# Four graph layers on one core: W a on TensorE, another beginning, and layer 2 projecting before it aggregates

## The chip, the cores and the metric

The kernel runs on one core of one Trainium2 chip. The metric is the device time of one execution in microseconds; the median of three runs is given. One execution was also recorded by the hardware profiler, and all views of the profile are of that one.

## The reference

There are 64 graphs of 256 nodes with 512 features. Each has an adjacency matrix `adj` (256 x 256) with positive weights and ones of its own on the diagonal. Four layers follow each other, each of the form `x = x + L(relu(layernorm(x)), adj)`. All is f32.

```
L0: Wh = h W0;  e[i,j] = leaky_relu((Wh a1)[i] + (Wh a2)[j]);  masked where adj <= 0.5
    att = softmax(e over i);   elu(att Wh)
L1: A = adj + I;  d = rsqrt(rowsum A);   relu((d A d) h W1 + b1)
L2: relu(adj h W2) * (row of h's input is not all zero)
L3: agg = (adj h) / max(rowsum adj, eps);   relu([h, agg] W3^T)
```

## The kernel before, in words

**One product.** A 256 x 256 result over 256 inner rows is formed by seven products of halves instead of eight, after Winograd. The seven left blocks are named A11, A12, S1, A22, S2, S4, S3, the seven right ones B11, B21, B22, T1, T2, T3, T4N. S and T are sums and differences of the other blocks. The weights' blocks (`wb[0]` to `wb[4]`, four layers and the two halves of W3) are made once at the beginning: `weight()` loads four blocks of 256 KB, `weight_sums()` makes T1 to T4N on GpSimd; `last_weight()` turns W3 by TensorE transposes.

**One graph.** `graph(b)` records the operations of a graph. `x` stays in the tile `xs`, the adjacency comes twice: `a_nat` as it is, for row sums, and by eight DMAs in blocks of 32 (`ab`) that VectorE turns into `aT`. A layer is: `norm(l)` (sums on GpSimd and ScalarE, then `h` on ScalarE); `aggregate(h, moving, l)`, which forms (A h)^T in two PSUM banks by 8 matmuls of 256 columns; `left_sums()`, which copies the four blocks into the tile `xw` (ScalarE, VectorE) and calls `more_sums()` for S2, S3 and S4 (VectorE, GpSimd); and `project()`, seven products with the layer's weights, each of two 128-row chunks, in three PSUM banks `pz`, `pv`, `py`. After a product, ScalarE copies a bank to a kept tile (`plain_keep`) or VectorE adds it to one (`plain_total`). Then comes the layer's nonlinearity and the addition to `xs` (`elu0`, `relu_add`, `masked`).

**Layer 0** makes the two logit vectors on VectorE as sums of `h0 * wa`, where `wa` holds W0 a. The first vector is needed along the free axis; `along()` brings it there: a small VectorE transpose, a DMA to DRAM (`dpl`) and a DMA back to all partitions (`pl`). `wa` itself is made at the beginning by `logit_weights()`: W0 is loaded once more, `a` is loaded in 128 copies, VectorE makes eight products with sums, and TensorE spreads the columns.

**Layer 3** projects before it aggregates. h^T is needed as left operand: VectorE transposes `h3` within blocks of 32 into `hb`, and 16 DMAs of 32 KB put the blocks in place in `hw`, in runs of 128 bytes. Then `hw` is multiplied by the neighbours' half of W3 (`wb[4]`, seven products) into the tile `y`, VectorE and GpSimd form y's T blocks, and seven products with 128-row blocks of `aT` and their sums `aw` (class `Gathered`) are accumulated into the same banks as the seven with `wb[3]`.

**Order.** Each operation is recorded with an engine, a declared time, and keys that it reads and writes. `Plan.place()` then walks through all operations of all graphs, with a list of buffers by tag, and fixes one static order per engine: the operation that can start first by the declared times (multiplied by `STRETCH`), then the urgent one, then the one with the earliest due time. Graph b's due time is `APART * b`, with an advance for the last `LAST` graphs. `SPARE` is added to a TensorE operation's ready time. All DMAs are issued by SyncE, in that order. So several graphs are under way at once, and TensorE's stream mixes their products.

Of the kernel before, what the change touches and what calls it, by code (L numbers as in the profile page):

```python
# [14 lines left out]
P = 128  # L15
Q = 32
# [6 lines left out]
APART = 12.0  # L23
LAST, LATE = 2, 0.3

STRETCH = {"DVE": 1.25, "ACT": 1.15, "POOL": 1.2, "PE": 1.0, "DMA": 1.0}
SPARE = 0.15
# [122 lines left out]
def kernel(  # L150
# [39 lines left out]
    class Tiles:  # L190
# [5 lines left out]
        def declare(self, name, shape, pool=None, tag=None):  # L196
            tag = pool or tag or name
            self.tiles[name] = Buffered(shape, tag, f"{name}_{self.name}")
# [43 lines left out]
    def spread(to, col):  # L242

        nc.tensor.transpose(to, col.to_broadcast([P, P]), ident)
# [8 lines left out]
    def logit_weights():  # L253
        me = Tiles("l", 0.0)
        op, declare = me.op, me.declare
        declare("wa_col", [P, 2, FC])
        for k in range(FC):
            declare(f"w0{k}", [P, O], tag="xw")
            op("DMA", 256, lambda g, k=k: nc.sync.dma_start(  # L259
                g[f"w0{k}"], w0[k * P : (k + 1) * P, :]), (), [f"w0{k}"])  # L260
        for j in range(2):
            declare(f"a{j}", [P, O], tag="ex512")
            op("DMA", 256, lambda g, j=j: nc.sync.dma_start(
                g[f"a{j}"],
                a0[j * O : (j + 1) * O, :].rearrange("o u -> u o").to_broadcast([P, O])),
               (), [f"a{j}"])
        for k in range(FC):
            for j in range(2):
                declare(f"junk{j}{k}", [P, O], tag="mva")
                op("DVE", 0.77, lambda g, j=j, k=k: nc.vector.scalar_tensor_tensor(  # L270
                    g[f"junk{j}{k}"], g[f"w0{k}"], 1.0, g[f"a{j}"], ALU.mult, ALU.mult,
                    accum_out=g["wa_col"][:, j, k : k + 1]),
                   [f"w0{k}", f"a{j}"], [f"junk{j}{k}", f"wa_col.{j}"])
        for j in range(2):
            declare(f"pw{j}", [P, F], "ps")

            def go(g, j=j):
                for k in range(FC):
                    spread(g[f"pw{j}"][:, k * P : (k + 1) * P], g["wa_col"][:, j, k : k + 1])

            op("PE", 0.6, go, [f"wa_col.{j}", "=ident"], [f"pw{j}"])
            op("ACT", 0.59, lambda g, j=j: nc.scalar.copy(wa[:, j, :], g[f"pw{j}"]),
               [f"pw{j}"], [f"=wa{j}"])

    def weight_sums(op, n, b12):
        w = wb[n]
        key = lambda i: b12 if i is None else f"=wb{n}.{i}"
        part = lambda g, i: g[b12] if i is None else w[:, i]
        for to, i, j in ((T1, None, B11), (T2, B22, T1), (T3, B22, None), (T4N, B21, T2)):
            op("POOL", 1.28, lambda g, to=to, i=i, j=j: nc.gpsimd.tensor_tensor(  # L290
                w[:, to], part(g, i), part(g, j), ALU.subtract),
               [key(i), key(j)], [key(to)])

    def weight(n, w):

        me = Tiles(f"w{n}", 0.0)
        me.declare("b12", [P, FH, OH], tag="hb")
        for at, i, j in ((B11, 0, 0), (None, 0, 1), (B22, 1, 1), (B21, 1, 0)):
            block = w[i * FH * P : (i + 1) * FH * P, j * OH : (j + 1) * OH].rearrange(
                "(k p) o -> p k o", p=P  # L300
            )
            me.op("DMA", 256, lambda g, at=at, block=block: nc.sync.dma_start(
                g["b12"] if at is None else wb[n][:, at], block),
                  (), ["b12" if at is None else f"=wb{n}.{at}"])
        weight_sums(me.op, n, "b12")

# [32 lines left out]
    def quarter(t, i, j):  # L339
        return t[:, i, j * OH : (j + 1) * OH]  # L340

    def graph(b):
# [82 lines left out]

        def more_sums(xw):
            put = lambda *n: [f"{xw}.{i}" for i in n]
            op("DVE", 0.43, lambda g: nc.vector.tensor_tensor(  # L428
                g[xw][:, S2], g[xw][:, S1], g[xw][:, A11], ALU.subtract),
               put(S1, A11), put(S2), urgent=True)  # L430
            for i, o in ((A22, S3), (A12, S4)):
                op("POOL", 0.85, lambda g, i=i, o=o: nc.gpsimd.tensor_tensor(  # L432
                    g[xw][:, o], g[xw][:, i], g[xw][:, S2], ALU.subtract),
                   put(i, S2), put(o), urgent=True)
# [39 lines left out]
        class Weighted:  # L474
# [5 lines left out]
            def left(self, g, at, k):  # L480
                return g[self.x][:, at, k]
# [114 lines left out]


# [34 lines left out]
        along("pl", lambda g: g["lg"][:, 0, :], ["lg.00", "lg.01"])  # L632
# [25 lines left out]
        aggregate("h0", "e", 0)  # L658
# [17 lines left out]
        project([Weighted("xw0", 0)], 0, plain_keep, 0.38, plain_total, lambda _: elu0(*first, "a"))  # L676
        elu0(*second, "b")
        elu0(*third, "c")
# [54 lines left out]
        aggregate("h2", "aT", 2)  # L733
# [12 lines left out]
        project([Weighted("xw2", 2)], 2, plain_keep, 0.38, plain_total, lambda _: masked(*first, "a"))  # L746
# [9 lines left out]

        declare("hb", [P, NC, F])
        for c in range(NC):
            op("DVE", 0.71, lambda g, c=c: nc.vector.transpose(g["hb"][:, c, :], g["h3"][:, c, :]),
               [f"h3.{c}"], [f"hb.{c}"])  # L760
        declare("hw", [P, 7, FH, P], tag="xw")
        parts = [(a, q) for a in range(P // Q) for q in range(P // Q)]
        for a, q in parts:
            op("DMA", 32, lambda g, a=a, q=q: nc.sync.dma_start(
                g["hw"][q * Q : (q + 1) * Q, : 2 * NC].rearrange("j s k n -> j (s k) n")[
                    :, :, a * Q : (a + 1) * Q],
                g["hb"][a * Q : (a + 1) * Q].rearrange("j c (k q r) -> q j (c k) r", q=P // Q, r=Q)[q]),
               ["hb.0", "hb.1"], [f"hw.{a}{q}"], holds=0.7)
        op("DVE", 0.43, lambda g: nc.vector.tensor_tensor(
            g["hw"][:, S1], g["hw"][:, S1], g["hw"][:, A22], ALU.add),  # L770
           [f"hw.{a}{q}" for a, q in parts], [f"hw.{i}" for i in (A11, A12, A22, S1)], urgent=True)
        more_sums("hw")

        declare("y", [P, 7, OH], tag="xw")
        declare("y12", [P, OH], tag="ex256")
        places = {(0, 0): (lambda g: g["y"][:, B11], f"y.{B11}"),
                  (0, 1): (lambda g: g["y12"], "y12"),
                  (1, 1): (lambda g: g["y"][:, B22], f"y.{B22}")}
        project([Weighted("hw", 4)], 4, plain_keep, 0.38, plain_total,
                lambda pz: op("ACT", 0.38, lambda g: nc.scalar.copy(g["y"][:, B21], g[pz]),  # L780
                              [pz], [f"y.{B21}"], urgent=True), places=places)
        for eng, us, to, i, j in (("DVE", 0.43, T1, None, B11), ("POOL", 0.85, T3, B22, None),
                                  ("DVE", 0.43, T2, B22, T1), ("DVE", 0.43, T4N, B21, T2)):
            name = lambda n: "y12" if n is None else f"y.{n}"
            of = lambda g, n: g["y12"] if n is None else g["y"][:, n]
            on = nc.vector if eng == "DVE" else nc.gpsimd
            op(eng, us, lambda g, on=on, to=to, i=i, j=j: on.tensor_tensor(
                g["y"][:, to], of(g, i), of(g, j), ALU.subtract), [name(i), name(j)],
               [f"y.{to}"], urgent=True)

        declare("aw", [P, 4, P], tag="mva")
        block = lambda g, c, i: g["aT"][:, c, i * P : (i + 1) * P]
        op("POOL", 0.5, lambda g: nc.gpsimd.tensor_tensor(
            g["aw"][:, 0], block(g, 0, 1), block(g, 1, 1), ALU.add), ["aT"], [f"aw.{S1}"])
        op("POOL", 0.5, lambda g: nc.gpsimd.tensor_tensor(
            g["aw"][:, 1], g["aw"][:, 0], block(g, 0, 0), ALU.subtract),
           ["aT", f"aw.{S1}"], [f"aw.{S2}"])
        for at, to, i in ((2, S3, 1), (3, S4, 0)):
            op("POOL", 0.5, lambda g, at=at, i=i: nc.gpsimd.tensor_tensor(
                g["aw"][:, at], block(g, 1, i), g["aw"][:, 1], ALU.subtract),  # L800
               ["aT", f"aw.{S2}"], [f"aw.{to}"])
        project([Weighted("hw", 3), Gathered("aT", "aw", "y")], 3, plain_keep, 0.38, plain_total,
# [9 lines left out]
    logit_weights()  # L812
# [4 lines left out]
    for b in range(B):  # L817
        graph(b)
    buffers = dict(
        xs=7, a_nat=1, ab=1, aT=6, h=3, mva=6, xw=5, c=3, off=1, junk=1, ex256=3, ex512=2,  # L820
        wa_col=1, turned=1, row=4, pl=1, pr=1, hb=1, ps=8,
# [37 lines left out]
```

## Time and profile before

| | |
|---|---|
| median of three runs | 2843.36 us (2842.63 to 2843.51) |
| profiled execution | 2844.11 us, its span 2842.3 us |
| granted TensorE clock, mean | 0.999 |
| PE / DVE / ACT / POOL busy | 2802.9 / 1963.5 / 1691.1 / 1246.4 us |
| matmul instructions | 12968 |
| mean busy share of the 16 DMA engines, queue q1 | 24.0% |
| moved | 161.07 MB in 495062 packets, 424816 of them under 512 B |
| SyncE: time of one h^T transfer's issue (`hw<-hb`, x1024) | 609 ns median |

PE is TensorE's matmul stream and PEld its weight loads, which overlap it; DVE is VectorE, ACT ScalarE, POOL GpSimd, SP SyncE. An f32 product is two matmul instructions, so instruction counts are twice the products of the code, but for the transposes. L529 is the line of the product matmuls in `project`, L460 that of `aggregate`. A tile's name in a row has its numbers left out: `hw` is h^T of layer 3, `xw` the aggregated and summed blocks of layers 0 to 2, `wa_col_l` and `junk_l` belong to `logit_weights`.

### The profile page before, as it was taken

How to read it: one execution, taken by the hardware profiler on the slowest of the kernel's cores; microseconds unless marked ns; L12 is line 12 of the kernel's file. 1: busy time of each engine (PE TensorE's matmuls, PEld its weight loads, DVE VectorE, ACT ScalarE, POOL GpSimd, SP SyncE). 2: the span in 40 equal slices, each digit the busy share in tenths (PEclk: the TensorE clock that was granted, in tenths of full speed). 3: DMA queues.
4: the chain of work that ended last, by engine and by line, in shares of the span. 5: the costliest groups of instructions: out<-in, count | busy, mean ns of one | idle time of the engine just before them, and what ended most of it. 6: DMA issues, size and time to landing. Idle time of an engine off the chain costs nothing.

```text
span 2842.3 us, 43136 instructions
## 1 busy us (share of the span) xinstructions
PE 2802.9 (99%) x12968; PEld 2461.2 (87%) x12968; DVE 1963.5 (69%) x5136; ACT 1691.1 (59%) x4115; POOL 1246.4 (44%) x2331
## 2 busy tenths in 40 slices
PE   5999999999999999999999999999999999999999
PEld 4888888888888888888888888888888888888887
DVE  7767676676766767667676667676776766667654
ACT  5766566556666566566565665665665656556552
POOL 6554344444444444444444444444444444443432
PEclk9999999999999999999999999999999999999999
DMA  7122331222222222222222222222222222222112
GB/s 199 20 51 61 72 70 40 62 53 53 58 53 58 56 49 59 61 45 61 46 62 56 47 66 55 48 59 56 53 59 47 60 53 40 58 49 44 39 34 52
DMA packets 495062, 161.07 MB, mean 57 GB/s; under 512 B 424816, under 2 KB 460656, under 8 KB 494832
## 3 DMA queue, kind: packets, MB, share of 16 engines
q1 hardware_dynamic: 494832, 158.33, 24.0%
q8 instruction: 105, 1.72, 0.3%
q14 instruction: 125, 1.02, 0.1%
HBM read 90.96 MB, written 33.69 MB: 44 GB/s over the span
## 4 chain that ended last, share of the span: by engine, by line
PE 97%; DMA 1%; DVE 1%; POOL 0%; SPq 0%; issue 0%; ACT 0%; DVEq 0%; POOLq 0%
PE pz L529 43%; PE pt L460 23%; PE pv L529 21%; PE py L529 11%; POOL wb L290 0%; DMA xs<-in_x_dram 0%; DMA ab<-in_adj_dram 0%; DVE e L628 0%; SPq L603 0%; DMA wb<-in_L_gnn_W_dram 0%; DVE e L642 0%; DMA pr<-dpr 0%; DVE xw L445 0%; SPq L259 0%; DVE stats L385 0%
## 5 line engine op out<-in xcount | busy, mean ns | idle before, releaser
L529 PE MATMUL pz<-wb,xw 128*128 128x256 f32 x3072 | 767.9, 379 | 2.5 <-DVE c L694 0.6
L529 PEld LDWEIGHTS pz<-wb,xw 128*128 128x128 f32 x3072 | 582.9, 190 | 83.9 <-ACT c L568 1.1
L568 ACT COPY c<-pz 128x256 f32<-128x256 f32 x576 | 213.6, 371 | 550.9 <-PE pz L529 550.3
L529 PE MATMUL pz<-wb,hw 128*128 128x256 f32 x2048 | 524.8, 379 | 0.9 <-ACT c L568 0.9
L432 POOL TENSOR_TENSOR xw<-xw 128x256 f32<-128x256 f32 x384 | 296.1, 791 | 482.1 <-DVE xw L428 326.5
L529 PEld LDWEIGHTS pz<-wb,hw 128*128 128x128 f32 x2048 | 389.0, 190 | 54.5 <-ACT c L568 1.7
L422 ACT ACTIVATE h<-xs,nb,rstd 128x512 f32<-128x512 f32 x512 | 402.1, 809 | 45.5 <-POOL nb L419 39.7
L529 PE MATMUL pv<-wb,xw 128*128 128x256 f32 x1536 | 393.7, 379 | 1.7 <-DVE xw L445 1.1
L529 PEld LDWEIGHTS pv<-wb,xw 128*128 128x128 f32 x1536 | 291.5, 190 | 41.9 <-POOL wb L290 1.5
L570 DVE TENSOR_TENSOR c<-pv,c 128x256 f32<-128x256 f32 x384 | 161.7, 421 | 222.3 <-PE pv L529 150.4
L401 ACT ACTIVATE h<-xs,mv 128x512 f32<-128x512 f32 x384 | 275.4, 718 | 56.1 <-POOL mv L395 36.3
L529 PE MATMUL pv<-wb,hw 128*128 128x256 f32 x1024 | 262.8, 379 | 0.0
L460 PE MATMUL pt<-e,h 128*128 128x256 f32 x1024 | 233.8, 381 | 15.8 <-ACT e L655 15.8
L460 PE MATMUL pt<-aT,h 128*128 128x256 f32 x1024 | 236.9, 379 | 0.0
L460 PE MATMUL pt<-ahT,h 128*128 128x256 f32 x1024 | 233.1, 379 | 0.0
L460 PEld LDWEIGHTS pt<-e,h 128*128 128x128 f32 x1024 | 195.8, 191 | 43.0 <-ACT e L655 16.1
L409 POOL TENSOR_TENSOR rstd<-rstd,minus_half 128x2 f32<-128x2 f32 x256 | 215.9, 843 | 17.3
L460 PEld LDWEIGHTS pt<-aT,h 128*128 128x128 f32 x1024 | 194.5, 190 | 26.7 <-ACT h L422 0.3
L460 PEld LDWEIGHTS pt<-ahT,h 128*128 128x128 f32 x1024 | 194.6, 190 | 26.5
L529 PEld LDWEIGHTS pv<-wb,hw 128*128 128x128 f32 x1024 | 194.5, 190 | 26.5
L628 DVE SCALAR_TENSOR_TENSOR e<-h,wa 128x512 f32<-128x512 f32 x256 | 196.7, 768 | 16.5 <-ACT h L422 5.8
L529 PE MATMUL py<-wb,xw 128*128 128x256 f32 x768 | 197.1, 379 | 0.0
(116 smaller groups left out, 4460.8 us busy)
## 6 DMA issues: line engine op xcount, KB each, us to landing
xs<-in_x_dram SPq DMA_DIRECT2D x64, 512.0 KB
hw<-hb SPq DMA_DIRECT2D x1024, 32.0 KB
out_dram<-xs SPq DMA_DIRECT2D x64, 512.0 KB
ab<-in_adj_dram SPq DMA_DIRECT2D x512, 32.0 KB
a_nat<-in_adj_dram SPq DMA_DIRECT2D x64, 256.0 KB
pl<-dpl SPq DMA_DIRECT2D x64, 128.0 KB
pr<-dpr SPq DMA_DIRECT2D x64, 128.0 KB
w3n_w<-in_L_gnn_W_dram SPq DMA_DIRECT2D x4, 512.0 KB
```

Of the source, the lines that this page charges most:

```text
L401: op("ACT", 1.0, lambda g, c=c: nc.scalar.activation(g[h][:, c, :], g["xs"][:, c, :], AF.Square, bias=g[mv][:, 0, c : c + 1], accum_out=g[ ...
L409: op("POOL", 0.72, lambda g: nc.gpsimd.tensor_tensor(g[rs], g[rs], minus_half, ALU.pow), [rs, "=half"], [rs])
L422: op("ACT", 0.81, lambda g, c=c: nc.scalar.activation(g[h][:, c, :], g["xs"][:, c, :], AF.Relu, bias=g[nb][:, c : c + 1], scale=g[rs][:, c ...
L432: op("POOL", 0.85, lambda g, i=i, o=o: nc.gpsimd.tensor_tensor(g[xw][:, o], g[xw][:, i], g[xw][:, S2], ALU.subtract), put(i, S2), put(o), ...
L460: nc.tensor.matmul(g[pt][:, kk, :], lhsT=g[h][:, c, k * P : (k + 1) * P], rhs=g[moving][:, c, :], start=(c == 0), stop=(c == NC - 1),)
L529: nc.tensor.matmul(g[t], lhsT=o.left(g, left, k), rhs=o.right(g, right, k), start=start and n == 0, stop=n == len(parts) - 1, skip_group_c ...
L568: return "ACT", lambda g, to, block: nc.scalar.copy(to, block)
L570: plain_total = (0.43, lambda g, i, to, block: nc.vector.tensor_tensor(to, block, to, ALU.add))
L628: op("DVE", 0.77, lambda g, j=j, c=c: nc.vector.scalar_tensor_tensor(g["e"].rearrange("p c n -> p (c n)"), g["h0"][:, c, :], 1.0, wa[:, j, ...
```

## The change

Five things change.

- W a: `logit_weights()` takes the blocks of W0 that are loaded anyway, transposes them on TensorE (16 transposes), loads `a` as eight rows of 128 (4 KB), transposes these, and forms W a by eight matmuls of 512 columns with a broadcast column as weights. The second load of W0, the 128 copies of `a` and VectorE's eight products go.
- The beginning: graphs 0 and 1 (`FIRST = 2`) do layer 0 in the other order: TensorE transposes h, the projection makes `wh`, and then two products of 512 columns for each half of the nodes aggregate it. Graphs 0 to 2 (`ON_PE = 3`) spread the logit row by two TensorE transposes in place of `along()`.
- Layer 2 does as layer 3's neighbours: `turn(2)` makes h^T by the DMAs, `neighbours(2, 2)` projects it with `wb[2]`, `block_sums` makes the sums of `aT`, and seven products `Gathered` aggregate. `aggregate` and `left_sums` of layer 2 go.
- `turn()`, for layers 2 and 3: VectorE's transposes write the two node halves woven (node 0 of half 0, node 0 of half 1, and so on), so that the 16 DMAs move runs of 256 bytes. The blocks A11, A12, S1 and A22 of `hw` therefore have a step of two words; S2, S3 and S4 are packed.
- The planner's constants and buffers: APART 12 to 16, LAST 2 to 4, LATE 0.3 to 0.5, STRETCH of DVE 1.25 to 1.15, of ACT 1.15 to 1.0, of POOL 1.2 to 1.25, SPARE 0.15 to 0.3; aT 6 to 7 buffers, mva 6 to 5, ex256 3 to 4, ex512 2 to 1.

```diff
+    def logit_weights(me):
+        OC = O // P
+        op("DMA", 4, lambda g: nc.sync.dma_start(
+            g["a_rows"], a0.rearrange("(r p) u -> r (p u)", p=P)), (), ["a_rows"])
+        op("PE", 0.15, lambda g: nc.tensor.transpose(
+            g["pa"], g["a_rows"], ident[: 2 * OC, : 2 * OC]), ["a_rows", "=ident"], ["pa"])
...
+                    nc.tensor.transpose(
+                        g[f"pw{i}"][:, k * P : (k + 1) * P], block[:, k % FH, o : o + P], ident)
...
+                op("PE", 0.9, lambda g, i=i, j=j: nc.tensor.matmul(
+                    g[f"pwa{j}"],
+                    lhsT=g["a_cols"][:, j * OC + i : j * OC + i + 1].to_broadcast([P, P]),
+                    rhs=g[f"wt{i}"], start=i == 0, stop=i == OC - 1,
...
+        def woven(t):
+            return t[:, : 4 * FH].rearrange("p b n -> p (b n)").rearrange(
+                "p (s k n i) -> p s k n i", s=2, k=FH, i=NC)
+        def left(t, at, k):
+            if len(t.shape) == 4:
+                return t[:, at, k]
+            if at < 4:
+                return woven(t)[:, at % 2, k, :, at // 2]
+            return t[:, at * FH + k]
...
+        def turn(l):
+            declare(hb, [P, F // Q, Q, NC], tag="hb")
+            for c in range(NC):
+                op("DVE", 0.71, lambda g, c=c: nc.vector.transpose(
+                    g[hb][:, :, :, c], g[h][:, c, :].rearrange("p (k r) -> p k r", r=Q)),
+                   [f"{h}.{c}"], [f"{hb}.{c}"])
+            declare(hw, [P, 7 * FH, P], tag="xw")
+            for a, q in parts:
+                op("DMA", 32, lambda g, a=a, q=q: nc.sync.dma_start(
+                    woven(g[hw])[q * Q : (q + 1) * Q, :, :, a * Q : (a + 1) * Q].rearrange(
+                        "j s k n i -> j (s k) (n i)"),
+                    g[hb][a * Q : (a + 1) * Q].rearrange("j (k q) r c -> q j k (r c)", q=P // Q)[q]),
+                   [f"{hb}.0", f"{hb}.1"], [f"{hw}.{a}{q}"], holds=0.42)
...
-        along("pl", lambda g: g["lg"][:, 0, :], ["lg.00", "lg.01"])
+        if b < ON_PE:
+            declare("pl", [P, N], "ps")
+            op("PE", 0.23, lambda g: [
+                spread(g["pl"][:, c * P : (c + 1) * P], g["lg"][:, 0, c : c + 1]) for c in range(NC)
+            ], ["lg.00", "lg.01", "=ident"], ["pl"])
+        else:
+            along("pl", lambda g: g["lg"][:, 0, :], ["lg.00", "lg.01"])
...
-        aggregate("h0", "e", 0)
+        if b < FIRST:
+                        nc.tensor.transpose(
+                            g[pt][:, k, c * P : (c + 1) * P], g["h0"][:, c, f0 : f0 + P], ident)
+            left_sums("pt0_0", "pt0_1", "xw0")
+            project([Weighted("xw0", 0)], 0, plain_keep, 0.38, plain_total, ..., places=places)
+            for i, piece in ((1, second), (0, third)):
+                        nc.tensor.matmul(g[po], lhsT=g["e"][:, c, i * P : (i + 1) * P],
+                            rhs=g["wh"][:, c, :], start=c == 0, stop=c == NC - 1)
...
-        aggregate("h2", "aT", 2)
+        turn(2)
+        neighbours(2, 2)
+        block_sums(2, "aT")
-        project([Weighted("xw2", 2)], 2, plain_keep, ...)
+        project([Gathered("aT", "aw2", "y2")], 2, plain_keep, ...)
...
+        turn(3)
+        neighbours(3, 4)
+        block_sums(3, "aT")
+        project([Weighted("hw3", 3), Gathered("aT", "aw3", "y3")], 3, plain_keep, ...)
```

## The prediction

> **What bounds the kernel now.** I read the busy row and the slices of the page first, then a table of stretches, then the waits of PE, then groups by shape, and last the start as a timeline.
>
> ```profile
> PE 2802.9 (99%) x12968; PEld 2461.2 (87%) x12968; DVE 1963.5 (69%) x5136; ACT 1691.1 (59%) x4115; POOL 1246.4 (44%) x2331
> PE   5999999999999999999999999999999999999999
> PEclk9999999999999999999999999999999999999999
> ```
>
> TensorE is full at full clock in 39 of 40 slices. No other engine is above 69%.
>
> ```profile
> 0.00:34.00 34.00, 4.56 (x10) 2.16 (x11) 21.27 (x55) 10.11 (x23) 17.23 (x25) 1.00 0.82 241
> 34.00:60.00 26.00, 23.18 (x104) 18.43 (x104) 24.14 (x52) 17.27 (x50) 21.59 (x31) 1.00 0.71 191
> 500.00:2500.00 2000.00, 2000.00 (x9268) 1760.61 (x9268) 1399.20 (x3663) 1201.76 (x2915) 867.39 (x1642) 1.00 0.24 54
> 2790.00:2843.00 53.00, 46.48 (x213) 39.93 (x212) 22.23 (x49) 11.38 (x28) 7.88 (x12) 0.97 0.23 60
> ```
>
> The columns after the length are PE, PEld, DVE, ACT, POOL (busy, instructions), then clock, DMA share and GB/s. Between 500 and 2500 us PE has no idle time: 2000 / 9268 = 0.2158 us for one 256-column matmul instruction. Each 256-column f32 product is two of them (x1024 in 64 graphs for the 8 products of an aggregation), so one product costs 0.4316 us. All 12928 layer instructions take 12928 x 0.2158 = 2789.9 us, the 32 transposes of W3 about 3.5 (eight took 0.87). The span of 2842.3 therefore holds 48.9 us that are not layer work, nearly all at its two ends.
>
> ```profile
> PE pt L460 <- ACT e L655: 15.8, 1, 15.8
> PE pw_l L244 <- DVE junk_l L270: 13.2, 5, 9.5
> ```
>
> These are PE's only long waits: for W a, and for the first attention matrix.
>
> **Steady state, the saving.** Layer 2 now aggregates (8 products of 256 columns) and then projects (7 x 2 = 14): 22. Changed, it projects (14) and gathers in seven products: 21. A graph goes from 101 to 100. In graphs 0 and 1 the aggregation of layer 0 becomes four products of 512 columns, equal to eight. So 64 x 0.4316 = 27.6 us leave the engine that has no gap.
>
> **What it adds, and what hides it.** All rows are per instruction of the same work in layer 3.
>
> ```profile
> L759 DVE STREAM_TRANSPOSE hb<-h 128x512 f32<-128x512 f32 x128 | 86.6, 693 | 0.3 <-ACT h L422 0.2
> L787 DVE TENSOR_TENSOR y<-y 128x256 f32<-128x256 f32 x128 | 80.0, 625 | 19.0 <-ACT y L780 16.2
> L787 POOL TENSOR_TENSOR y<-y,y 128x256 f32<-128x256 f32 x64 | 61.1, 955 | 55.8 <-DVE y L570 52.5
> L529 PEld LDWEIGHTS pz<-wb,hw 128*128 128x128 f32 x2048 | 389.0, 190 | 54.5 <-ACT c L568 1.7
> L244 PEld LDWEIGHTS pw_l<-ident,wa_col_l 128*128 128x128 f32 x8 | 1.4, 181 | 15.6 <-issue 9.5 <-DVE junk_l L270 6.1
> ```
>
> DVE gains per graph two transposes (1.4), three additions into y (3 x 0.42), three differences (2 x 0.625 + 0.43) and slower block sums (0.596 + 0.567 for 0.414 + 0.455, +0.3): 4.6 us. It had 1963.5 / 64 = 30.7 of 44.4 us and gets 35.3 of about 43.2, 82%. ACT gains four copies of 0.371 and loses 0.589 + 0.372: +0.5, to 62%. POOL gains T3 (0.955) and the four sums of a^T (0.507 + 0.473 + 2 x 0.55): +3.0, to 52%. None reaches PE, so I price them at 0. If the cover fails, each 0.1 us of PE waiting per graph costs 6.4 us.
>
> The transposes write, and the block sums and weight loads read, every second word now. No row of before has such an access. For DVE and POOL the ends are the same time and double: the transposes of layers 2 and 3 would add 2.8 us, DVE would be at 88%, still below PE.
>
> SP issues 32 transfers of h^T per graph in place of 16. One holds it for a median of 609 ns now, at 256 runs of 128 bytes; the row vector pl, 128 runs, holds it 368. With 128 runs of 256 bytes I take 0.37 to 0.61: 11.8 to 19.5 us in place of 9.7. The rest of SP's issues is about 7 us (ab 3.8 in the timeline, seven others at 0.35 to 0.57), so at most 26.5 of 43.2. What stands behind them on SP is x, ab and a_nat of later graphs, with about a graph's time of lead. The DMA engines are at 24%; the number of packets of h^T stays, their size doubles. Even at double time per packet they would not pass 40%.
>
> The Trainium skill, "DMA: Bandwidth & Descriptors" (Specifications), speaks against runs this short: line rate needs 512 bytes or more. By it both 128 and 256 are poor. No row here separates the two, and at this share it would change no term.
>
> Does the new latency of layer 2 fit? From layer 1's last sum: relu 0.73, POOL mean 0.38, two squares 1.8, POOL 0.24 + 0.84 + 0.22, two h 1.6, two transposes 1.4, 16 issues 5.9 to 9.7, landing 3.5 (last issue over at 1004.25, first sum on hw at 1007.70), sum 0.6: 17 to 21 us, some 3 more for hand-overs. In the changed order at least 34 us of other graphs' PE instructions stand there for graphs 6 to 57 (count x 0.2158), and 30 ahead of layer 3. From the neighbours' last v product to T2's use lie at least 3.0 us; the need is 0.42 + 0.43 + 0.62 and hand-overs, about 2. It fits, but with far less room than at the turn.
>
> **The start.**
>
> ```profile
> 16.01 0.25 DVE L355 STREAM_TRANSPOSE tpl<-lg 128x64 f32<-128x64 f32 x1
> 21.88 0.34 SPq L361 DMA_DIRECT2D pl<-dpl  x1
> 26.22 0.91 ACT L634 ACTIVATE e<-pl,lg 128x256 f32<-128x256 f32 x2 [0.34 <-DMA pl<-dpl]
> 33.20 5.62 PE L460 MATMUL pt<-e,h 128*128 128x256 f32 x16 [15.84 <-ACT e L655]
> ```
>
> Now the first layer work begins at 33.2; the row of logits alone travels 10 us through DRAM. Changed, W0 is loaded once and not twice, a as 4 KB and not 512 KB: 1.8 MB stand up to graph 0's ab, at 241 GB/s about 8 us plus issue, and I put ab at 12 and h at 14.6 (now 14.9). PE's W a costs 17 transposes at 0.11 and eight 512-column products of 0.863, 8.8 us, all in idle time; it ends near 17, no earlier than now (18.0). DVE loses eight products of 0.68, 5.4 us. The gain is elsewhere: eight transposes of h (0.9) and the projection can run from 18 to 25 while the softmax is made, and the logits take two spreads (0.47 each in the row of the eight for W a) in place of the 10 us. In the changed order e waits behind aT of graph 1 on DVE (its ab cannot be issued before graph 0's aT is read, so near 21), then min, top, exp, division, with two h of graph 1 between: ready near 28.5. The two 1.7 us aggregations follow.
>
> By 60 us PE now has done about 87 layer instructions and 20 transposes, 21 us of work. Changed, I count by then two projections of layer 0 (12), their aggregations (6.9), the next layer 0 and two layer 1 aggregations (10.4), one projection of layer 1 (6) and the W3 transposes (3.5): 38.8. That is 17.8 us ahead. DVE was 24.14 of 26 busy from 34 to 60 and has more to do per graph now, so part is given back before steady state. Ends: 0 and 18. I take 11.
>
> **The end.** The last PE product now feeds an addition (0.42) and a 512-wide relu (0.69) before the store; changed, its last feeds one relu of 0.42: -0.7. The last four graphs are packed otherwise, and layer 2 has a longer chain there: +0 to +6, with new short gaps elsewhere; I take +2.
>
> **Sum.** 2844.1 (profiled execution; its span is 2842.3, 1.8 around it) - 27.6 - 11 - 0.7 + 2 = 2806.8. The median of the runs lies 0.75 lower: 2806.
>
> **Rivals.** *Strided weights, slower than before.* Left blocks A11, A12, S1 and A22 are loaded with every second word: 4 of 7 products, two chunks, two instructions, three projections, 48 instructions per graph, 3072 in all. A load takes 190 ns under a matmul step of 215.8. It is free up to there; beyond, each pays the excess. It eats the whole gain at 215.8 + 39.3 / 3.072 = 229 ns, a load 20% longer; at double, 380, it costs 504 us: 3310. Against it: the load of a broadcast column, step 0, took 181, not more than a packed one. I take 0, the row nearest to it being any load there is. Chance 0.08.
> The Trainium skill, "SBUF — State Buffer" (the note on 16-byte cachelines), says that reads keep full speed while two fall in one line, for f32 up to a step of 8 bytes or so; by it this price is 0. No run here shows it yet.
>
> *DVE's queue.* At 82% and in order, an addition that PE's next product needs may come late in every graph. For: the ends above. Against: apart from W a, PE waited for DVE 2.4 us in all of before. With 0.2 to 0.4 us per graph the time is 2819 to 2832 (0.08); over 0.6 it is no gain or worse (0.07, of which 0.02 stay within the bound).
>
> *The new beginning brings nothing*, since DVE is the bound until 100 us: 2806 + 11 = 2817. Chance 0.15.
>
> **Numbers.** The forecast itself 0.62. What a measurement can tell from no change is about 0.2%, 5.7 us. Faster 0.62 + 0.15 + 0.08 = 0.85; same 0.02; slower 0.05 + 0.08 = 0.13. The range goes from 18 us at the start and no cost at the end (2806 - 7 - 2 = 2797, three less for that sum's errors) to near the end of the late-DVE case: 2794 to 2830.
>
> **What would show it.** 100 products per graph and a step of 215.8 ns with no idle PE between 500 and 2500; loads on hw of 190 ns; layer work of graph 0 before 20 us and the first aggregation near 28; DVE near 82%. It is wrong if loads on hw pass 216 ns, if PE's waits name DVE y or DMA hw by the hundred, or if PE shows gaps after 100 us.

## The result and the profile after: 7% slower, with gaps in front of layers 2 and 3

The changed kernel takes 3043.43 us (median of 4 runs, 3042.51 to 3047.97) against 2843.2: a ratio of 1.0707, interval 1.0691 to 1.0722. The forecast was 2806. The profiled execution took 3043.74 us, its span is 3041.9, the mean granted clock 0.991.

The busy row, TensorE's slices and the shares of the chain that ended last, from the page of the changed kernel:

```profile
PE 2857.0 (94%) x12871; PEld 2456.7 (81%) x12871; DVE 2157.4 (71%) x5623; ACT 1718.8 (57%) x4246; POOL 1450.0 (48%) x2653
PE   8899899999999999999999999999999999999998
...
SPq 36%; PE 33%; DVE 10%; DMA 8%; issue 6%; POOL 4%; ACT 3%; DVEq 0%; ACTq 0%; POOLq 0%
```

The slices hide it: a nine stands for 90% and up. The busy row shows it: TensorE has 3041.9 - 2857.0 = 184.9 us of idle time where before had 39.4. That is +145.5; the other 54.1 of the 199.6 us by which the span grew are busy time, although there are fewer instructions. Part of that goes with the clock (0.991 where before had 0.999; 0.8% of 2857 is 23 us, an estimate). The rest is longer instructions, the products on h^T among them (389 ns in the mean, 379 in the run with four transfers below); how it divides is not shown. The chain says more: SyncE's issues hold 36% of it. In before TensorE held 97%.

The stretch of 2000 us that had no gap before:

```profile
500.00:2500.00 2000.00, 1900.40 (x8629) 1643.26 (x8628) 1447.33 (x3797) 1151.10 (x2850) 954.57 (x1770) 1.00 0.29 63
```

With 200 instructions to a graph, a graph takes 2000 / 8629 x 200 = 46.4 us. Without gaps it would take 200 x 0.2158 = 43.2; before it took 43.6. So the saving per graph is there and 3.2 us lie on top, 2.3 of gaps and 0.9 of longer instructions, 64 times over: 205 us.

What TensorE, SyncE's queue and VectorE wait for (total us, times, longest):

```profile
PE pzy L565 <- DMA hw<-hb: 116.4, 87, 3.1
PE pzy L565 <- ACT y L604: 15.1, 14, 1.4
PE pzy L565 <- issue: 9.8, 17, 1.4
```

```profile
SPq L645 <- PE pz L565: 358.6, 67, 11.5
SPq L907 <- DVE xs L847: 219.9, 41, 13.5
SPq L645 <- DVE hb L639: 206.6, 47, 12.5
```

```profile
DVE hw L650 <- DMA hw<-hb: 470.4, 127, 5.7
```

`pzy` are the first products on h^T, and they wait 87 times for its transfers. That comes near the "by the hundred" that the prediction named as a sign against it, and the gaps after 100 us, another of its signs, are there. The second table tells what SyncE's queue waits for. 47 times a turn waits for VectorE's transposes of h, which the prediction had counted. 67 times it waits for a TensorE product: `hw` shares its five buffers (`xw`) with the aggregated blocks and with `y`, and SyncE can't write into one before the last product has read its former contents. The row of L907 is the wait for a finished graph before it is stored. The last row is the largest wait for the transfers: in 127 of 128 turns VectorE comes to the first sum on `hw` before the data and stands there, 3.7 us in the mean. Its work for the other graphs, and the next transposes of h with it, stands behind that sum. In before the same wait was 4.3 us in all.

One turn in the order of time (start, length, engine, line):

```profile
1035.01 1.31 DVE L639 STREAM_TRANSPOSE hb<-h 128x512 f32<-128x512 f32 x2
...
1038.04 10.26 SPq L645 DMA_DIRECT2D hw<-hb  x16
...
1049.93 0.43 DVE L650 TENSOR_TENSOR hw<-hw 128x256 f32<-128x256 f32 x1 [4.43 <-DMA hw<-hb]
1049.96 1.11 PE L565 MATMUL pzy<-wb,hw 128*128 128x256 f32 x4 [0.83 <-DMA hw<-hb]
```

h^T is transposed in its blocks at 1036.3; SyncE then waits 1.6 us for a `pz` product, the issue begins at 1038.0 and lasts 10.3 us, and the last piece lands 1.6 us after it. VectorE has stood for 4.4 us and TensorE for 0.8, and both start at once. The order was built for 16 x 0.42 = 6.7 us of issue. One transfer takes:

```profile
L645 SPq DMA_DIRECT2D hw<-hb x2048: 585/599/1861, 87.8 to 3011.4; - x187
```

599 ns median (between minimum and maximum), where the 256 runs of 128 bytes of before took 609. Half the number of runs made it 2% shorter. The `holds=0.42` of the diff is what the planner was told; before told it 0.7 for 0.609.

### The profile page after: what moved, and what is told of

It reads as the page before. It is cut to its first block, busy times and chain, and to the rows that moved or that the text cites. A ratio compares the mean times of both kernels' runs of the same rounds, so it can differ in the third digit from the quotient of the medians.

```text
span 3041.9 us, 45682 instructions
## 1 busy us (share of the span) xinstructions
PE 2857.0 (94%) x12871; PEld 2456.7 (81%) x12871; DVE 2157.4 (71%) x5623; ACT 1718.8 (57%) x4246; POOL 1450.0 (48%) x2653
## 4 chain that ended last, share of the span: by engine, by line
SPq 36%; PE 33%; DVE 10%; DMA 8%; issue 6%; POOL 4%; ACT 3%; DVEq 0%; ACTq 0%; POOLq 0%
SPq L645 36%; PE pz L565 8%; PE pzy L565 8%; DMA hw<-hb 7%; PE pt L496 7%; PE pv L565 4%; PE pvy L565 3%; PE py L565 2%; DVE xs L847 1%; DVE hb L639 1%; DVE hw L650 1%; DVE hw L464 1%; DVE xs L768 1%; ACT h L436 1%; PE pyy L565 1%
## 5 line engine op out<-in xcount | busy, mean ns | idle before, releaser
L565 PE MATMUL pzy<-wb,hw 128*128 128x256 f32 x2048 | 542.2, 389 | 145.5 <-DMA hw<-hb 116.4
L565 PEld LDWEIGHTS pzy<-wb,hw 128*128 128x128 f32 x2048 | 385.3, 194 | 242.2 <-issue 138.5
L565 PE MATMUL pz<-wb,xw 128*128 128x256 f32 x2048 | 520.0, 380 | 7.1 <-ACT wh L604 1.9
L468 POOL TENSOR_TENSOR hw<-hw 128x256 f32<-128x256 f32 x256 | 219.7, 878 | 559.8 <-DVE hw L464 374.7
L565 PEld LDWEIGHTS pz<-wb,xw 128*128 128x128 f32 x2048 | 388.4, 190 | 63.9 <-POOL xw L468 2.4
L650 DVE TENSOR_TENSOR hw<-hw 128x256 f32<-128x256 f32 x128 | 54.6, 427 | 475.2 <-DMA hw<-hb 470.4
L565 PE MATMUL pvy<-wb,hw 128*128 128x256 f32 x1024 | 267.1, 384 | 0.0
L565 PE MATMUL pz<-wb,hw 128*128 128x256 f32 x1024 | 263.5, 380 | 0.1
L604 ACT COPY y<-pzy 128x256 f32<-128x256 f32 x384 | 139.6, 363 | 179.0 <-PE pzy L565 162.6
L565 PEld LDWEIGHTS pvy<-wb,hw 128*128 128x128 f32 x1024 | 200.3, 196 | 24.6
L565 PEld LDWEIGHTS pz<-wb,hw 128*128 128x128 f32 x1024 | 198.2, 194 | 24.6 <-ACT c L604 0.5
```

The costliest lines, as they stand in the source:

```text
L565: nc.tensor.matmul(g[t], lhsT=o.left(g, left, k), rhs=o.right(g, right, k), start=start and n == 0, stop=n == len(parts) - 1, skip_group_c ...
L604: return "ACT", lambda g, to, block: nc.scalar.copy(to, block)
L650: op("DVE", 0.48, lambda g: nc.vector.tensor_tensor(block(g[hw], S1), block(g[hw], S1), block(g[hw], A22), ALU.add), [f"{hw}.{a}{q}" for a ...
```

## Experiments

**Theory A**: the transfers hold SyncE 0.60 us each, the order is built on 0.42, and the difference, 16 times per turn, twice per graph, closes a loop through the shared buffers. **Theory B**: strided writes and reads or VectorE's load are the cause. **Theory C**: five `xw` buffers are too few for six tiles per graph, whatever the speed of the transfers.

### The same order, with a quarter of the transfers

```diff
+            def move(g, a, q):
+                if q == P // Q - 1:
+                    nc.sync.dma_start(
+                        g[hw][:, a * FH : (a + 1) * FH].rearrange("p k n -> p (k n)"),
+                        g[hb][:, a * 4 : (a + 1) * 4].rearrange("p k r c -> p (k r c)"))
```

> The changed kernel with the same order on PE, DVE, ACT and POOL, but each turn of h is moved by 4 transfers of 128 KB (128 runs of 1 KB) in place of 16 of 32 KB; they carry the same bytes to wrong places of hw, so the values of layers 2 and 3 are not the reference's. Theory A (SyncE needs 0.60 us for each of the 16 issues where the order was built on 0.42, so every turn's data come about 3 us after the place that the order gives them, and TensorE waits there twice per graph): issue falls from 9.6 to about 2 us per turn, the waits on hw vanish, 2810 to 2830 us. Theory B (the extra VectorE work and its in-order queue, or the accesses with a step of two words, slow every graph): nothing changes, 3000 us or more. Theory C (too few buffers for hw and y, whatever the speed of the transfers): between, above 2900.

This kernel leaves out putting the blocks in their places, so it computes other values in layers 2 and 3. 2821.14 us (2819.82 to 2821.7), ratio 0.9921 (0.9906 to 0.9936). The stretch, the transfers and the weight loads on `hw`, and one turn's issue:

```profile
500.00:2500.00 2000.00, 2000.00 (x9268) 1774.73 (x9267) 1556.33 (x4077) 1244.11 (x3033) 999.02 (x1895) 1.00 0.23 67
```

```profile
L646 SPq DMA_DIRECT2D hw<-hb x512: 464/595/1915, 88.6 to 2781.2; - x171
L565 PEld LDWEIGHTS pzy<-wb,hw x2048: 190/192/198, 98.3 to 2810.0; 128*128 128x128 f32 x187
```

```profile
1012.83 2.45 SPq L646 DMA_DIRECT2D hw<-hb  x4
```

Everything that theory B blames is still there: the same strided accesses of the engines, VectorE at 1556 / 2000 = 78%, the same order and the same five buffers. TensorE has no gap. B falls, and C as it was put, whatever the speed of the transfers. A sixth buffer was not tried, so what the five buffers add to the loss at sixteen transfers is not shown. The order of TensorE, VectorE, ScalarE and GpSimd that the change brought is a good one as soon as the turn is short. Here SyncE waits for `pz` even longer than in the changed kernel, 620.1 us in all: the wait for the buffer by itself costs nothing; it puts the start of the turn where its length decides.

VectorE's wait for `hw` is gone as well: its list of waits has no such row. A transfer of 128 KB in 128 runs of 1 KB takes 595 ns to issue. In the three shapes measured here the time follows neither the runs nor the bytes.

### Twelve transfers

```diff
+                if q == 2:
+                    return
+                lo = q * Q if q < 2 else 2 * Q
+                hi = lo + (Q if q < 2 else 2 * Q)
+                src = g[hb][a * Q : (a + 1) * Q] if q < 2 else g[hb][2 * Q :]
```

> As four, the same order on PE, DVE, ACT and POOL, but 12 transfers per turn (8 of 32 KB and 4 of 64 KB to wrong places; layers 2 and 3 are not the reference's). At 0.6 us each they take 7.2 us where the order gives 16 x 0.42 = 6.7. Theory A: the delay per turn is about 0.5 in place of 2.9 us, most of the loss is gone: 2821 to 2860. Theory C, or a cost that goes with the number of transfers by itself: about half to three quarters of the loss stays, 2930 to 2990.

2829.07 us (2826.97 to 2829.49), ratio 0.9949 (0.9934 to 0.9964). One turn and the stretch:

```profile
1013.75 7.99 SPq L650 DMA_DIRECT2D hw<-hb  x12
```

```profile
500.00:2500.00 2000.00, 1998.79 (x9252) 1770.63 (x9251) 1559.52 (x4071) 1237.28 (x3030) 1008.82 (x1894) 1.00 0.31 67
```

This kernel too leaves blocks in wrong places, but the bytes of a turn (512 KB) and the runs (256 bytes) are those of the changed kernel. So it was not these that made the 3043 us: the number of issues is what differs. The turn's issue takes 7 to 8 us, already over the 6.7 of the plan, and the steady stretch has 1.2 us of gaps. With 4, 12 and 16 transfers in one order the times are 2821, 2829 and 3043. That is no straight line: four transfers more beyond twelve cost 214 us, eight fewer gain 8. The order gives the turn somewhere between the 8.0 us that still fit and the 9.6 or more (16 x 0.6) that do not (an estimate), and what exceeds that is paid in every graph. VectorE's wait for `hw`, 141.4 us here, costs TensorE next to nothing at this size.

### All sixteen, declared as they are

```diff
-                   [f"{hb}.0", f"{hb}.1"], [f"{hw}.{a}{q}"], holds=0.42)
+                   [f"{hb}.0", f"{hb}.1"], [f"{hw}.{a}{q}"], holds=0.62)
```

> The changed kernel with one number altered: the declared issue time of an h^T transfer is 0.62 us and not 0.42, which is what the traces show (0.599 to 0.609). The instructions are the same, only the fixed orders differ. Theory A: the order now leaves the room that the transfers need; 2815 to 2850 us, with few waits on hw. Theory B: no change, 3000 or more. Theory C (the turn's latency with five xw buffers can't be hidden by any order): above 2900.

2863.76 us (2863.2 to 2866.84), ratio 1.0074 (1.0059 to 1.0089): one number takes back 180 of the 200 us. It lies 14 us above the range that I gave for theory A, and 36 below that of theory C.

```profile
100.00:250.00 150.00, 132.17 (x582) 112.57 (x582) 95.82 (x252) 88.03 (x226) 69.62 (x129) 0.95 0.27 62
500.00:2500.00 2000.00, 2000.00 (x9267) 1773.97 (x9266) 1553.81 (x4074) 1261.98 (x3039) 1005.75 (x1904) 1.00 0.30 67
2700.00:2862.00 162.00, 144.32 (x642) 123.47 (x642) 87.06 (x203) 61.56 (x146) 52.96 (x96) 0.98 0.24 51
```

All 32 transfers per graph are issued at their real speed and the steady stretch is full: 9267 instructions at 200 to a graph are 43.16 us. What remains lies at the ends: 17.8 us idle from 100 to 250, 11.2 of them in two waits for `hw`, and 17.7 in the last 162, where only a few graphs are left to cover a turn. This order differs from that of the changed kernel everywhere, so the run shows that a true declared time is enough, not which operations moved.

### Does a lower declared time help by itself?

```diff
 # before
-                ["hb.0", "hb.1"], [f"hw.{a}{q}"], holds=0.7)
+                ["hb.0", "hb.1"], [f"hw.{a}{q}"], holds=0.55)
```

> The kernel before with one number altered: the declared issue time of an h^T transfer is 0.55 us and not 0.7 (measured 0.609), so that the order is built on turns that are 0.9 us shorter than they are. Theory A: PE begins to wait for hw here too, but by less than 1 us per graph: 2845 to 2900 us. Theories B and C: as before, within 0.2%, 2838 to 2849.

2847.13 us (2845.74 to 2848.35, 10 runs), ratio 1.0013 (1.0003 to 1.0022). 0.06 us too little, with one turn per graph, costs 3.6 us. This lies in the range of theory A and in that of the other two, so it does not decide between them. VectorE's wait for `hw` rose from 4.3 to 77.6 us.

### Layer 2 put back

```diff
-        turn(2)
-        neighbours(2, 2)
-        block_sums(2, "aT")
+        aggregate("h2", "aT", 2)
...
-        project([Gathered("aT", "aw2", "y2")], 2, plain_keep, ...)
+        project([Weighted("xw2", 2)], 2, plain_keep, ...)
```

> The changed kernel with layer 2 as before (aggregation by PE, then projection): 16 woven transfers per graph, 101 products, the new beginning and constants kept. Theory A: one turn per graph is left with its under-declared issue time, so part of the loss stays at most: 2830 to 2900 us. If the beginning gains the 11 us of the prediction and layer 3's turn has room, 2831. Theory B: close to 2832, since the extra DVE work is gone.

3143.78 us (3140.14 to 3154.13), ratio 1.1062 (1.1043 to 1.1082). This is 244 us above the top of the range that I expected (2830 to 2900). With half the transfers the kernel is still slower.

```profile
500.00:2500.00 2000.00, 1860.08 (x8297) 1607.07 (x8298) 1238.52 (x3282) 1073.52 (x2605) 783.03 (x1480) 0.97 0.21 49
```

```profile
PE pt L496 <- ACT h L436: 94.6, 18, 6.0
PE pzy L565 <- DMA hw<-hb: 72.6, 32, 5.2
```

Besides h^T, TensorE now waits for ScalarE's h. Of these 2000 us, 140 are gaps; an instruction takes 0.2242 us where it took 0.2158, at a granted clock of 0.97, and that makes another 70. The buffer has little part in it: SyncE waits 63.8 us for `pz`, where the changed kernel waited 358.6. VectorE's wait for `hw` is 253.9 us in 61 turns. Theory A alone does not explain this kernel. The kernel still has the new beginning, the new constants and buffers, and the declared 0.42. The next two take these apart in part.

### The beginning and the woven transfers alone

Layer 2, the planner's constants, the buffers and `holds=0.7` are those of before; `logit_weights`, `FIRST = 2`, `ON_PE = 3` and `turn(3)` are those of the change.

```diff
 # before
+ON_PE = 3
+FIRST = 2
...
-        declare("hb", [P, NC, F])
...
+        turn(3)
+        neighbours(3, 4)
+        block_sums(3, "aT")
```

> The new beginning (W a by PE, graphs 0 and 1 projecting first, logits of graphs 0 to 2 by PE) and the woven transfers of layer 3, but layer 2 by aggregation and the planner's constants, buffers and declared issue time (0.7) of before. If the beginning gains what the prediction took, 2832 us; if its PE work (about 12 us of W a, transposes and spreads) eats what the earlier projection gains, within 5 us of 2843. If the 3144 us of l2_back came from the beginning or the woven layout and not from the constants, 2900 or more.

2846.59 us (2843.55 to 2849.09, 11 runs), ratio 1.0011 (1.0002 to 1.0019). Neither the beginning nor the weave explains the 3144, and the beginning gains nothing. Where it falls behind:

```profile
80.00:100.00 20.00, 16.61 (x59) 13.49 (x60) 13.47 (x44) 13.19 (x33) 10.82 (x18) 0.74 0.13 27
```

```profile
82.72 3.78 PE L496 MATMUL pt<-ahT,h 128*128 128x256 f32 x8 [4.82 <-ACT h L436]
```

These 20 us hold 59 matmul instructions where before had 95, at a granted clock of 0.74. After a wait of 4.82 us, eight of them take 3.78 us; eight of the same shape at 62.09 took 1.89. By 100 us the layer work done is 50.9 us (236 instructions of 256 columns by 0.2158) against 56.3 in before.

### The same with the low declared time

```diff
-                   [f"{hb}.0", f"{hb}.1"], [f"{hw}.{a}{q}"], holds=0.7)
+                   [f"{hb}.0", f"{hb}.1"], [f"{hw}.{a}{q}"], holds=0.42)
```

> The kernel of the run with the new beginning and the woven transfers of layer 3 alone (layer 2, constants and buffers of before; 2846.6 us), with one number changed: the declared time of SyncE per h^T transfer 0.42 in place of 0.7. The transfers really hold SyncE about 0.60 us. It asks what made the kernel with layer 2 put back (3143.8 us) slow, which had this declared time and also the new constants and buffers. If the declared time alone is to blame (theory A with one turn per graph): over 3000 us, PE pzy waiting for DMA hw by dozens, fewer than 8700 matmul instructions from 500 to 2500 us. If the new constants and buffers are to blame and one understated turn per graph has room enough: 2840 to 2870 us and above 9150 instructions in that stretch. A time between, 2870 to 3000, would share the blame. I expect the last of these to be the least likely and lean to the second, 0.55 to 0.35, since with one turn per graph SyncE has 11.8 us of these transfers to issue in 43.6.

2899.31 us (2895.34 to 2900.66), ratio 1.0193 (1.0176 to 1.021).

```profile
500.00:2500.00 2000.00, 1973.63 (x9055) 1731.84 (x9054) 1335.67 (x3582) 1171.97 (x2847) 859.10 (x1611) 0.99 0.23 53
```

It fell in the band that I had thought least likely. The number alone costs 2899.3 - 2846.6 = 52.7 us with one turn per graph. It accounts for 52.7 of the 297 us by which the kernel with layer 2 put back lies above the one without the new constants. The other 244 belong to the constants and buffers, or to these together with the number. Which of them stays open: no run separates them.

### A version that beats both

```diff
-APART = 16.0
+APART = 15.8
+BACK = 3
-LAST, LATE = 4, 0.5
+LAST, LATE = 3, 0.4
-SPARE = 0.3
+SPARE = 0.25
...
-                   [f"{hb}.0", f"{hb}.1"], [f"{hw}.{a}{q}"], holds=0.42)
+                   [f"{hb}.0", f"{hb}.1"], [f"{hw}.{a}{q}"], holds=0.6)
...
+        turned2 = b < B - BACK
+        if turned2:
+            turn(2)
+            neighbours(2, 2)
+            block_sums(2, "aT")
+        else:
+            aggregate("h2", "aT", 2)
```

> The changed kernel with a declared issue time of 0.60 us per h^T transfer, layer 2 of the last three graphs by the old aggregation, and APART 15.8, LAST 3, LATE 0.4, SPARE 0.25. Theory A: no waits for hw in the middle, and the tail's waits go too: 2815 to 2830 us, below the kernel before. If the layer's latency can't be hidden (theory C), or the DVE queue costs (theory B): 2845 or more.

2825.71 us (2823.43 to 2826.89, 5 runs), ratio 0.9935 (0.9923 to 0.9948).

```profile
500.00:2500.00 2000.00, 2000.00 (x9268) 1774.20 (x9267) 1587.45 (x4075) 1247.16 (x3037) 1038.88 (x1894) 1.00 0.31 67
...
2770.00:2821.00 51.00, 47.12 (x218) 41.42 (x216) 22.56 (x48) 7.82 (x21) 5.64 (x7) 1.00 0.22 59
```

All transfers are those of the changed kernel. The three last graphs aggregate first in layer 2, so they have one turn less where little is left to cover it, and the last 51 us are 92% busy. Several things changed at once here, against the run with a declared 0.62 (2863.76 us); what each of them brings is not shown.

## Why the prediction was wrong, point by point

**Right.** The saving of 27.6 us and the step of 0.2158 us: the kernels with 4 transfers, with a declared 0.62, and the last one all do 9267 or 9268 instructions in 2000 us, at 200 to a graph. The strided weight loads at no price: 192 ns in the median and 198 at most in the row above, under the 215.8 of a matmul step. Here the note on 16-byte cachelines in the Trainium skill's "SBUF — State Buffer", cited in the prediction, held: a step of two f32 words costs next to nothing. VectorE's load: 78 to 79% where 82 was predicted, and no gap from it in these kernels. Both rivals are refuted as causes; but VectorE's queue, which the second one named, carries the delay where the transfers come late.

**The step that failed** is "Does the new latency of layer 2 fit?", with its answer "It fits". It had three errors.

First, it counted 17 to 21 us from layer 1's last sum, as if a transfer could start once h^T is in `hb`. 67 times it starts later, when TensorE lets go of a buffer. The prediction priced SyncE as occupancy, "at most 26.5 of 43.2", and asked only what stands behind the transfers on its queue. It did not ask what they wait for themselves. With `y` and `hw` twice per graph, a graph now takes six tiles from the five `xw` buffers, where it took five, so a late turn can hold up the next: product, free buffer, sixteen issues, landing, product. The issues are the 36% of SyncE in the chain. The latencies by themselves do not show the loss: with the wait for the buffer, 5.4 us in the mean of the 67, the prediction's 24 become 29, still under the 34 that were counted as cover. That cover was counted as if the order stood still; but it was an order made for turns of 6.7 us.

Second, the sum on `hw` was put at 0.6 us and VectorE's standing in front of it at nothing. It stood there 470.4 us, and what it does for other graphs waited with it. Per turn this wait is 0 to 1.2 us in the kernels whose steady stretch is full or nearly so, and 2.7 (the low declared time with one turn), 3.7 (the changed kernel) and 4.0 (layer 2 put back) in the three that lose time there. How the loss divides between the buffer and VectorE's queue is read from the waits and not separated by a run.

Third, the price of an issue was taken as 0.37 to 0.61 us, with its lower end from `pl`, a transfer from DRAM. It was 0.599, at the end that came from the transfer of the same kind. The diff showed 0.42 in its place, and the two were not compared. The ends of this range times 16 (5.9 and 9.7 us) lie on either side of the 8.0 us that still fit in the run with 12. So the range held the answer, and the sum of latencies did not let it decide anything. The landing of 3.5 us was misread, on the safe side: the sum at 1007.70 had not waited for the data, and the landing measured above is 1.6.

**The beginning, -11, was mis-sized**; with the woven transfers and nothing else it measured +3.0 (2846.59 against 2843.59). The single events came about as predicted: the first projection at 19.59 us (18 predicted), the first aggregation at 29.77 (28.5). By 60 us the changed kernel had done 25.9 us of layer work against 19.0, in 256-column instructions times 0.2158, where 35.3 were predicted. By 100 us it had 51.8 against 56.3. The stretch in which it is lost:

```profile
60.00:80.00 20.00, 19.31 (x92) 16.66 (x92) 19.20 (x47) 16.21 (x40) 16.16 (x23) 1.00 0.26 54
80.00:100.00 20.00, 9.86 (x37) 7.32 (x36) 13.91 (x38) 10.15 (x29) 11.39 (x16) 0.83 0.28 61
```

```profile
92.27 5.27 PE L496 MATMUL pt<-e,h 128*128 128x256 f32 x16 [6.63 <-ACT e L755]
```

VectorE is at 96% up to 80 us, and then TensorE waits 6.6 us for the attention matrix of graph 3. That graph's logits are the first that travel through DRAM, but they are not what is late: `pl` is issued at 73.86, and VectorE is busy for all of the 6 us from 86 to 92. After the wait sixteen instructions take 5.27 us, where sixteen at 64.75 took 3.62. The third rival, "the new beginning brings nothing, since DVE is the bound until 100 us", was right in its effect. It was given 0.15.

**The end** was to cost 2 - 0.7. It is not separately measured. With four transfers the profiled execution lies 23.2 us below before's: -27.6 for the products and +4.4 for both ends together. How these divide in this order is not shown.

**The chance of slower, 0.13,** went to strided weights and VectorE's queue. The mechanism that happened stood in the text only as a sign, "DMA hw by the hundred", and had no place, price or chance. With 1.6 us of excess per turn (46.4 - 43.2 over two turns) it would have been 3.2 x 64 = 205 us.

## What to carry to other kernels

In a static order, a transfer that is declared too short costs nothing until it outlasts its slack; beyond that point it is paid in every round, if the next round waits for it, through a shared buffer or through the queue of an engine that stands at its data. Price an added group of transfers as one stretch, issues times the time of one of the same kind plus landing, from the moment its buffer is free, and compare that with what the planner was told. A share of SyncE's time says nothing about it.

## What the hardware showed that I had not expected

- The issue of an SBUF to SBUF transfer took about 0.6 us in all three shapes: 609 ns at 256 runs of 128 bytes, 599 at 128 runs of 256, 595 at 128 runs of 1 KB. From DRAM the eight of `ab` took 3.80 us in the timeline, 475 ns each. `pl` (128 runs, from DRAM) had a median of 368 ns in before, but 588 in the changed kernel: 0.59 us at 1048.34, right behind a turn, and 0.34 at 1086.49. So the issue time of one and the same transfer can change with its place; why is not shown.
- The granted clock stays near 1.00 in the mean of the steady stretch of the changed kernel (95% busy, its waits for `hw` 1.3 us in the mean), but falls to 0.83 (49% busy) and 0.74 (83% busy) in single stretches of 20 us near the beginning, and to 0.97 on average in the kernel with layer 2 put back, 93% busy with waits of up to 6 us. The eight instructions that took 3.78 us in place of 1.89 after a wait of 4.82 show it singly: a gap can cost more than its own length.
